# Two cross-attention layers on one core: eleven of layer 1's sixteen rotary chains are transposed by VectorE and on a way through DRAM

## The chip, the core and the metric

The kernel runs on one NeuronCore of a Trainium2 chip. A core has five engines that each work through a queue of their own in order: TensorE (PE, matrix products into PSUM), VectorE (DVE), ScalarE (ACT), GpSimd (POOL) and SyncE (SP), which here only issues DMA transfers. They wait for each other on semaphores. A DMA is waited for in the same way: whoever needs the data, or the buffer that a transfer reads, waits until it has landed. The metric is the device time of one execution in microseconds (us); a kernel is run several times and the median is taken.

## The reference

Four batches of 1024 rows pass through two cross-attention layers, everything in float32. Layer 0 normalises `x`, projects it to 16 heads of 64, attends to a context of 1024 rows and adds the projected result to `x`. Layer 1 does the same with 16 heads of 32, but its q and k are rotated and scaled to unit length before they meet:

```python
xn = x * rsqrt(mean(x * x) + EPS_RMS) * norm_w
q = (xn @ wq).reshape(B, T_dec, N_HEADS, HEAD_DIM)
k, v = split((encoder_out @ wkv).reshape(B, T_enc, 2, N_HEADS, HEAD_DIM))
q, k = rotate(q, cos, sin), rotate(k, cos, sin)
q, k = q / norm(q), k / norm(k)
attn = softmax(einsum("bqhd,bkhd->bhqk", q, k) * sqrt(HEAD_DIM))
out = residual + einsum("bhqk,bkhd->bqhd", attn, v).reshape(B, T_dec, D_Q) @ wout
```

## The kernel before, in words

The batches follow each other. In each, layer 0 works through eight pairs of heads (`Attention0`, L354), and then layer 1 through two halves of eight heads each (`Attention1`, L555). Everything that is not attention itself, such as projections, transposes and sums, is cut into units with an estimated PE cost in us. The `Units` object (L56) holds them in a list, and after each attention step `fill` (L70) issues as many as the step's share of cost allows, in the list's order. So the order of every engine's queue is settled when the program is built. A unit that costs 0.0 is issued as soon as it is reached while the step still owes time.

A half of layer 1 has 32 steps, counted here from 0 (steps of the second half go on from 32). A step (`att1.step`, L571) handles one block of 256 query columns, one group of four heads and two blocks of 128 keys: eight score matmuls (L581), two exps on ACT (L591) into one of two buffers, the eight products of the step before (L626), the units (`fill`, L595), and then two adds on VectorE that begin the softmax sums (L600), with a third (L602) in two of four steps. Each block of queries and group takes four steps; the second step of the next block holds the eight matmuls that end the sums (L645). A step's scores need the PSUM tiles of the step before, so its exps must be done. The query block changes every eight steps: steps 0, 8, 16 and 24 begin with columns 0, 256, 512 and 768 of q. PE writes two records for one such matmul, so that 16 records are eight matmuls.

Before they can meet in scores, q and k must lie with the head's dimension on partitions. `rotated_chains` (L452) makes them. A batch has sixteen chains: four each for k and q of the first half and of the second (`k`, `q` in the first, `k1`, `q1` in the second), each with 256 rows. A chain has three parts:

- `project` (L463): matmuls into one PSUM bank, rows on partitions; at the last, `rotate` (L475) is issued: a square on ACT (L478), five instructions on VectorE (L480 to L485), and on POOL the norm's inverse root (L487, L169) and the scaling (L491). The result is `t1`, 128 partitions x 512.
- nothing in the second place.
- `turn_over` (L494), cost 0.45: four PE transposes of 128x128 into a PSUM bank (L499) and one ACT copy into the q or k tile (L504).

`weave` (L96) puts a chain's turn two chains behind its projection. `t1` comes from `Scratch` (L525), which hands out four slots in turn, so a slot is written again four chains later. Marks (L859) make sure that the turns of q are issued before steps 8, 16 and 24 at the latest.

All DMA issues concerned here are on SP, in program order. During the first half of layer 1 SP has, before the change: the weights `wo1` for the second half (L863, `wo_load`, L653), then the next batch's weights `w` (L303) and context rows `c` (L176). The `wo1` weights are first used by the units `po1` in the fill of step 32, and the next batch's context rows in step 33 and after.

Of the kernel before, what the change touches and what calls it, by code (L numbers as in the profile page):

```python
# [29 lines left out]
F32 = mybir.dt.float32  # L33
AF = mybir.ActivationFunctionType
# [3 lines left out]
P = 128  # L38
S = 1024
NT = S // P  # L40
DQ = 512
NQ = DQ // P
DC = 384
NC_ = DC // P
# [4 lines left out]
HD1 = 32  # L49
# [60 lines left out]
def xattn_kernel(ctx: ExitStack, tc: tile.TileContext, a: dict, out: bass.AP):  # L110
    nc = tc.nc
    x, c = a["x"], a["ctx_768"]
# [3 lines left out]
    sb = ctx.enter_context(tc.tile_pool(name="sb", bufs=2))  # L116
    ps_s = ctx.enter_context(tc.tile_pool(name="ps_s", bufs=2, space=bass.MemoryType.PSUM))
    ps_f = ctx.enter_context(tc.tile_pool(name="ps_f", bufs=1, space=bass.MemoryType.PSUM))
    ctx.enter_context(tc.manual_schedule())

    def score(name, shape=(P, S)):
# [5 lines left out]
    def bank(name):  # L127

        while True:
            which["n"] = which["n"] + 1 if which["n"] < 3 else which["from"]  # L130
            if which["n"] != which["kept"]:
                break
            which["kept"] = None
        return ps_f.tile([P, 512], F32, tag=f"f{which['n']}", name=name)
# [25 lines left out]
    def matmul(o, lhsT, rhs, start, stop):  # L160

        w = P // which["cols"]
        for j in range(which["cols"]):
            rr = slice(j * w, (j + 1) * w)
            nc.tensor.matmul(o[rr], lhsT[:, rr], rhs, start=start, stop=stop)  # L165

    def rsqrt(o, v):

        nc.gpsimd.tensor_tensor(o, v, nhalf[:, : v.shape[1]], ALU.pow)  # L169
# [268 lines left out]
    TH = 2  # L438

    def half_kv_load(half, i):  # L440
        f0, f1 = half * FH, (half + 1) * FH
        w = sb.tile([P, NC_, FH], F32, tag=f"wkv{i}", bufs=1, name=f"wkv{i}_{half}")
        nc.sync.dma_start(w, a["wkv"][:, i * DQ + f0 : i * DQ + f1].rearrange("(n p) m -> p n m", p=P))
        return w

    def half_q_load(half):
        f0, f1 = half * FH, (half + 1) * FH
        wq = sb.tile([P, NQ, FH], F32, tag="wpair", bufs=2, name=f"wq1_{half}")
        nc.sync.dma_start(wq, a["wq"][:, f0:f1].rearrange("(n p) m -> p n m", p=P))
        return wq  # L450

    def rotated_chains(dst, src, nk, w, name, tmp):  # L452

        hd, nh = HD1 // 2, TH * FH // HD1
        tiles = {}

        def heads(ap):
            return ap.rearrange("p (t h d) -> p t h d", t=TH, d=HD1)

        def spread(ap):  # L460
            return ap.unsqueeze(2).to_broadcast([P, TH, FH // HD1, ap.shape[2]])

        def project(t0, i, k):  # L463
            if i == 0 and k == 0:
                tiles[t0] = [bank(f"{name}_p{t0}")]
                if which["from"] == 0:
                    which["kept"] = which["n"]
            pp = tiles[t0][0]
            t = t0 + i
            lhsT = src[t // 4][:, k, (t % 4) * P : (t % 4 + 1) * P]  # L470
            matmul(pp[:, i * FH : (i + 1) * FH], lhsT, w(k), k == 0, k == nk - 1)
            if i == TH - 1 and k == nk - 1:
                rotate(t0, pp)

        def rotate(t0, pp):  # L475

            t1, t2, sq = tmp.take()
            nc.scalar.activation(sq, pp, AF.Square)  # L478
            c_, s_ = cos[:, t0 : t0 + TH, :], sin[:, t0 : t0 + TH, :]
            nc.vector.tensor_mul(heads(t1), heads(pp), spread(c_))  # L480
            nc.vector.tensor_mul(heads(t2)[:, :, :, :hd], heads(pp)[:, :, :, hd:], spread(s_[:, :, :hd]))
            nc.vector.tensor_mul(heads(t2)[:, :, :, hd:], heads(pp)[:, :, :, :hd], spread(s_[:, :, hd:]))
            nc.vector.tensor_add(t1, t1, t2)
            ss = sb.tile([P, nh], F32, tag="ss", bufs=2, name=f"{name}_s{t0}")
            nc.vector.tensor_reduce(ss, sq.rearrange("p (h d) -> p h d", d=HD1), AX.X, ALU.add)  # L485
            sm = sb.tile([P, nh], F32, tag="sm", bufs=2, name=f"{name}_m{t0}")
            nc.gpsimd.tensor_scalar_max(sm, ss, EPS_L2 * EPS_L2)  # L487
            ri = sb.tile([P, nh], F32, tag="ri", bufs=2, name=f"{name}_r{t0}")
            rsqrt(ri, sm)
            t1h = t1.rearrange("p (h d) -> p h d", d=HD1)  # L490
            nc.gpsimd.tensor_mul(t1h, t1h, ri.unsqueeze(2).to_broadcast([P, nh, HD1]))  # L491
            tiles[t0] = t1

        def turn_over(t0):  # L494
            t1 = tiles.pop(t0)
            pt = bank(f"{name}_t{t0}")
            for g in range(2):
                for i in range(TH):
                    nc.tensor.transpose(  # L499
                        pt[:, (g * TH + i) * P : (g * TH + i + 1) * P],  # L500
                        t1[:, i * FH + g * P : i * FH + (g + 1) * P],
                        ident,
                    )
            nc.scalar.copy(dst()[:, :, t0 * P : (t0 + TH) * P], pt.rearrange("p (g t) -> p g t", g=2))  # L504

        return [
            (
                [(0.44, lambda t0=t0, i=i, k=k: project(t0, i, k)) for i in range(TH) for k in range(nk)],
                [],
                [(0.45, lambda t0=t0: turn_over(t0))],  # L510
            )
            for t0 in range(0, NT, TH)
        ]

    def qk_tile(name):
        return sb.tile([P, 2, S], F32, tag="qk", bufs=3, name=name)
# [196 lines left out]
    st, order = prepare_units(0)  # L713
# [14 lines left out]
    for b in range(B):  # L728
        ct, hT, pairs = st["ct"], st["hT"], st["pairs"]
# [6 lines left out]
        for p in range(NPAIR):  # L736
# [22 lines left out]
            if p == 6:  # L759
                kq = {}  # L760

                def begin(n, kq=kq, b=b):
                    kq[n] = qk_tile(f"{n}1_{b}_0")

                k = rotated_chains(lambda kq=kq: kq["k"], ct, NC_, lambda k, wk=wk: wk[:, k, :], f"k1_{b}_0", RowScratch())
                other = [(0.0, lambda: begin("k"))] + k[0][0] + flat(outs[:2]) + k[1][0] + k[0][2] + flat(outs[2:4])
            if p == NPAIR - 1:
# [4 lines left out]
                xnT = []  # L772
# [7 lines left out]
                wk1 = []  # L780
# [4 lines left out]
            n = 7 * (p == 0)  # L785
# [6 lines left out]
            if p == 5:  # L792
                wq = []
                work.add([(0.0, lambda wq=wq: wq.append(half_q_load(0)))])
            left = sum(c for c, _ in values) if p == NPAIR - 1 else 0.0
            for i in range(NT):
# [8 lines left out]
                n = NT * (NPAIR - p) - i  # L805
# [13 lines left out]
        tmp = Scratch(b)  # L819
        wv1, wq1 = half_kv_load(1, 1), half_q_load(1)  # L820
        begin("q")
        kT, qT = kq["k"], kq["q"]
        kT1, qT1 = qk_tile(f"k1_{b}_1"), sb.tile([P, 2, S], F32, tag="raw", bufs=1, name=f"q1_{b}_1")
        q = rotated_chains(lambda kq=kq: kq["q"], xnT, NQ, lambda k, wq=wq: wq[0][:, k, :], f"q1_{b}_0", tmp)
        k1 = rotated_chains(lambda kT1=kT1: kT1, ct, NC_, lambda k, wk1=wk1: wk1[0][:, k, :], f"k1_{b}_1", tmp)
        q1 = rotated_chains(lambda qT1=qT1: qT1, xnT, NQ, lambda k: wq1[:, k, :], f"q1_{b}_1", tmp)

        work.add(flat(outs[:4]) + norms[0]["stats"] + k1[0][0] + [(AV, att.product)] + norms[0]["apply"])
        work.add(norms[0]["turn"] + q[0][0] + k1[1][0] + k1[0][2] + [(AV, att.product)] + flat(outs[4:]) + q[0][2])
# [14 lines left out]
        for half in range(2):  # L844
            n = 0
# [14 lines left out]
            else:  # L860
# [4 lines left out]
                if b + 1 < B:  # L865
                    st, order = prepare_units(b + 1)
# [75 lines left out]
```

## Time and profile before

| | us |
|---|---|
| median of 3 runs | 2908.89 |
| lowest and highest run | 2907.53, 2913.90 |
| the profiled execution | 2903.31 |
| its span, first to last instruction | 2901.5 |
| PE busy in the span | 2849.7 |
| VectorE busy | 2189.1 |
| layer 1, first half, first batch | 497.65 to 624.34 |

The profile comes from one execution. It lists instructions by engine and line, with busy time and what ended the idle time ahead of them (`<-`). `PE q_t` and `PE k_t` are the transposes of `turn_over`, `q_p` and `k_p` the projections, `rot` is `t1` and its companions, `s` a score tile, `both` the softmax sums, `po` an output projection. A matmul's end is modelled, so start times of consecutive instructions tell more than durations. "SPq" rows are DMA issues. For a DMA the profile tells packets, bytes, and the time from issue to landing.

### The profile page before, as it was taken

The page shows a single profiled execution, that of the slowest core. Times are in us where ns is not written, and L with a number is a line of the kernel's source. Part 1 is how long each engine was busy: PE and PEld are TensorE (multiplying, and loading weights), DVE is VectorE, ACT ScalarE, POOL GpSimd, SP SyncE. Part 2 cuts the span into 40 slices and gives each one's busy share as a digit, 9 for nine tenths or more (in the row PEclk, how much of TensorE's full clock was granted, in tenths as well). Part 3 has the DMA queues.
Part 4 walks back from the last instruction along what each step waited for, and adds up shares of the span by engine and source line. Part 5 has one row for each costly group of instructions (what it writes and reads, how often), then busy time and mean ns, then how long its engine had stood idle before and what let it go on. Part 6 is the DMA issues. An engine that isn't in the chain of part 4 may idle for free.

```text
span 2901.5 us, 66687 instructions
## 1 busy us (share of the span) xinstructions
PE 2849.7 (98%) x27336; PEld 1425.7 (49%) x27336; DVE 2189.1 (75%) x2952; ACT 1439.5 (50%) x2329; POOL 938.9 (32%) x776
## 2 busy tenths in 40 slices
PE   8999999999999999999999999999999999999998
PEld 4444455555444444555544445455554444445544
DVE  5677785877777778587777777858877777786877
ACT  4444444666444444466644444446664444444665
POOL 2343353420134335432024433534102343353400
PEclk9999999999999999999999999999999999999999
DMA  5887775010398777401039887730104887773000
GB/s 144 189 187 181 167 171 133 22 37 25 75 210 192 183 170 175 113 22 36 26 92 211 192 184 166 178 93 22 36 26 112 207 197 183 165 171 81 2 2 30
DMA packets 177552, 348.87 MB, mean 120 GB/s; under 512 B 37600, under 2 KB 93152, under 8 KB 177248
## 3 DMA queue, kind: packets, MB, share of 16 engines
q1 hardware_dynamic: 175920, 343.96, 50.1%
q8 instruction: 216, 3.54, 0.5%
q14 instruction: 88, 0.72, 0.1%
q10 hardware_dynamic: 1328, 0.66, 0.1%
HBM read 67.64 MB, written 8.39 MB: 26 GB/s over the span
## 4 chain that ended last, share of the span: by engine, by line
PE 89%; DVE 4%; ACT 3%; issue 2%; SPq 1%; DMA 1%; POOL 1%; DVEq 0%; ACTq 0%
PE s L367 16%; PE av L428 15%; PE po L165 11%; PE s L581 9%; PE pv L165 8%; PE pqT L165 7%; PE av L626 7%; PE pkT L165 5%; PE q_p L165 4%; PE k_p L165 2%; PE av L645 2%; ACT e L591 1%; SPq L412 1%; PE pth L247 1%; DMA eT<-e 1%
## 5 line engine op out<-in xcount | busy, mean ns | idle before, releaser
L392 DVE TENSOR_REDUCE m<-s 128x1 f32<-128x1024 f32 x512 | 602.9, 1219 | 372.1 <-PE s L367 371.5
L591 ACT ACTIVATE e<-s 128x1024 f32<-128x1024 f32 x512 | 496.7, 1022 | 252.5 <-PE s L581 239.5
L398 POOL TENSOR_SCALAR raw<-raw,li 128x1024 f32<-128x1024 f32 x256 | 287.1, 1122 | 725.0 <-DVE li L397 717.0
L367 PE MATMUL s<-qk 64*128 64x512 f32 x2048 | 515.6, 615 | 2.9 <-ACT e L393 2.2
L393 ACT ACTIVATE e<-s,m 128x1024 f32<-128x1024 f32 x256 | 283.1, 1110 | 465.8 <-DVE m L392 224.2
L393 ACT ACTIVATE raw<-s,m 128x1024 f32<-128x1024 f32 x256 | 285.4, 1115 | 455.0 <-DVE m L392 455.0
L428 PE MATMUL av<-eT,v 128*64 128x256 f32 x4096 | 470.1, 382 | 4.8 <-DMA eT<-e 3.6
L398 POOL TENSOR_SCALAR e<-e,li 128x1024 f32<-128x1024 f32 x256 | 287.0, 1122 | 473.7 <-DVE li L397 244.2
L600 DVE TENSOR_TENSOR both<-e 128x512 f32<-128x512 f32 x512 | 340.5, 699 | 87.2 <-ACT e L591 84.3
L428 PEld LDWEIGHTS av<-eT,v 128*64 128x64 f32 x4096 | 284.7, 137 | 225.1 <-issue 84.8
L367 PEld LDWEIGHTS s<-qk 64*128 64x128 f32 x2048 | 183.7, 186 | 281.6 <-issue 165.9
L581 PE MATMUL s<-q,k 32*128 32x256 f32 x4096 | 306.0, 401 | 5.8 <-ACT q L504 2.7
L401 DVE STREAM_TRANSPOSE e<-e 128x1024 f32<-128x1024 f32 x256 | 310.0, 1229 | 0.3
L401 DVE STREAM_TRANSPOSE e<-raw 128x1024 f32<-128x1024 f32 x256 | 310.0, 1228 | 0.2 <-DMA eT<-e 0.2
L581 PEld LDWEIGHTS s<-q,k 32*128 32x128 f32 x4096 | 192.1, 184 | 141.0 <-ACT e L591 72.0
L165 PE MATMUL pqT<-hT,w 128*64 128x512 f32 (+1 forms) x1216 | 240.6, 595 | 2.5 <-ACT hT L249 2.5
L165 PE MATMUL po<-wo,vals 128*64 128x512 f32 x1024 | 234.6, 596 | 0.0
L295 DVE TENSOR_TENSOR x<-x,po 128x512 f32<-128x512 f32 x200 | 131.7, 678 | 86.2 <-PE po L165 85.2
L165 PEld LDWEIGHTS pv<-w,cT 128*64 128x64 f32 (+1 forms) x3360 | 170.3, 132 | 41.6 <-issue 34.8
L165 PE MATMUL pv<-w,cT 128*64 128x128 f32 (+1 forms) x3360 | 184.3, 274 | 0.7 <-ACT hT L249 0.7
L165 PE MATMUL pkT<-cT,w 128*64 128x512 f32 (+1 forms) x912 | 182.4, 598 | 0.0
L602 DVE TENSOR_TENSOR both<-both 128x1024 f32<-128x1024 f32 x128 | 159.7, 1248 | 4.4
(82 smaller groups left out, 2776.1 us busy)
## 6 DMA issues: line engine op xcount, KB each, us to landing
eT<-e SPq DMA_DIRECT2D x2048, 128.0 KB, 2.4
xr<-in_x_dram SPq DMA_DIRECT2D x32, 256.0 KB, 4.0
wo<-in_Wo_dram SPq DMA_DIRECT2D x16, 512.0 KB, 4.5
x<-in_x_dram SPq DMA_DIRECT2D x32, 256.0 KB, 4.0
out_dram<-x SPq DMA_DIRECT2D x32, 256.0 KB, 2.6
w<-in_Wq_dram SPq DMA_DIRECT2D x31, 256.0 KB, 3.2
c<-in_ctx_dram SPq DMA_DIRECT2D x32, 192.0 KB, 4.2
wkv<-in_wkv_dram SPq DMA_DIRECT2D x16, 384.0 KB, 3.5
```

Source lines behind the costliest of these rows:

```text
L165: nc.tensor.matmul(o[rr], lhsT[:, rr], rhs, start=start, stop=stop)
L367: nc.tensor.matmul(sc[j][:, kb * 512 : (kb + 1) * 512], pr["qT"][r[j], i * P : (i + 1) * P], pr["kT"][r[j], kb * 512 : (kb + 1) * 512], st ...
L392: nc.vector.tensor_reduce(m[:, j : j + 1], sc[j], AX.X, ALU.max, negate=True)
L393: nc.scalar.activation(e[j], sc[j].rearrange("p (g s) -> p g s", g=4), AF.Exp, bias=m[:, j : j + 1], accum_out=l[:, j : j + 1])
L398: nc.gpsimd.tensor_scalar(e[j], e[j], li[:, j : j + 1], HD0**-0.5, ALU.mult, ALU.mult)
L401: self.turn = [lambda j=j: nc.vector.transpose(self.e[:, :, i % BQ * 2 + j, :], e[j]) for j in range(2)]
L428: nc.tensor.matmul(av[r[j], :W].rearrange("p (t a i) -> p t a i", t=BQ, a=4), pr["v"][:, k, r[j]], eT[:, j, :, :, k * 32 : (k + 1) * 32], ...
L581: nc.tensor.matmul(sc[j // 2][:, j % 2, c, :], kT[rr, g, k * P : (k + 1) * P], qT[rr, g, qb * WQ : (qb + 1) * WQ], start=True, stop=True,)
L591: nc.scalar.activation(e, sc[u], AF.Exp, scale=float(np.sqrt(np.float32(HD1))))
L600: nc.vector.tensor_add(into[:, 2 * u : 2 * u + 2, :], es[u][:, :, 0, :], es[u][:, :, 1, :])
L602: nc.vector.tensor_add(acc, acc, into)
L626: nc.tensor.matmul(self.av[rr, 0, :], v[g][:, 2 * kk + c, rr], es[j // 2][:, j % 2, c, :], start=first and c == 0, stop=end and c == 1,)
```

## The change

`rotated_chains` takes a new argument, `blocks_from`. Chains whose first row block is at or behind it have a new turn. All four `k1`, all four `q1` and the last three `q` chains of a batch have it: eleven of sixteen, 44 in all. The five others (the four of `k` and the first of `q`) keep `turn_over`.

For the eleven, `rotate` writes its result with heads ahead of row blocks, which changes access patterns only. The turn has two units of cost 0.0. `turn_blocks` transposes `t1` in place in 32x32 blocks on VectorE, and writes it to a DRAM tile in four transfers, one for each group of 32 partitions, in pieces of 32 elements. `put_blocks` reads it back into the q or k tile in four transfers, one for each head of the four, in pieces of 256 elements. All eight are issued by SP. There are four DRAM tiles in turn. PE and ACT have no part in it.

```diff
+    dram = ctx.enter_context(tc.tile_pool(name="dram", bufs=4, space=bass.MemoryType.DRAM))
...
-    def rotated_chains(dst, src, nk, w, name, tmp):
+    def rotated_chains(dst, src, nk, w, name, tmp, blocks_from=NT):
...
-        def heads(ap):
-            return ap.rearrange("p (t h d) -> p t h d", t=TH, d=HD1)
+        def heads(ap, t0=-1):
+
+            order = "p (h t d) -> p t h d" if t0 >= blocks_from else "p (t h d) -> p t h d"
+            return ap.rearrange(order, t=TH, d=HD1)
...
-            nc.scalar.activation(sq, pp, AF.Square)
+            nc.scalar.activation(heads(sq, t0), heads(pp), AF.Square)
...
-            nc.vector.tensor_mul(heads(t1), heads(pp), spread(c_))
-            nc.vector.tensor_mul(heads(t2)[:, :, :, :hd], heads(pp)[:, :, :, hd:], spread(s_[:, :, :hd]))
-            nc.vector.tensor_mul(heads(t2)[:, :, :, hd:], heads(pp)[:, :, :, :hd], spread(s_[:, :, hd:]))
+            h1, h2 = heads(t1, t0), heads(t2, t0)
+            nc.vector.tensor_mul(h1, heads(pp), spread(c_))
+            nc.vector.tensor_mul(h2[:, :, :, :hd], heads(pp)[:, :, :, hd:], spread(s_[:, :, :hd]))
+            nc.vector.tensor_mul(h2[:, :, :, hd:], heads(pp)[:, :, :, :hd], spread(s_[:, :, hd:]))
...
+        def turn_blocks(t0):
+            t1 = tiles.pop(t0)
+            nc.vector.transpose(t1, t1)
+            way = dram.tile([HD1, 2, 4, TH, P], F32, tag="way", name=f"{name}_w{t0}")
+            for a in range(4):
+                to = way.rearrange("d g h t (a x) -> a d (g h t) x", a=4)[a]
+                nc.sync.dma_start(to, t1[32 * a : 32 * (a + 1)].rearrange("d (n x) -> d n x", x=32))
+            tiles[t0] = way
+
+        def put_blocks(t0):
+            way = tiles.pop(t0)
+            for h in range(4):
+                to = dst()[32 * h : 32 * (h + 1), :, t0 * P : (t0 + TH) * P]
+                nc.sync.dma_start(to, way[:, :, h].rearrange("d g t x -> d g (t x)"))
+
...
-                [(0.45, lambda t0=t0: turn_over(t0))],
+                [(0.0, lambda t0=t0: turn_blocks(t0)), (0.0, lambda t0=t0: put_blocks(t0))]
+                if t0 >= blocks_from
+                else [(0.45, lambda t0=t0: turn_over(t0))],
...
-        q = rotated_chains(lambda kq=kq: kq["q"], xnT, NQ, lambda k, wq=wq: wq[0][:, k, :], f"q1_{b}_0", tmp)
-        k1 = rotated_chains(lambda kT1=kT1: kT1, ct, NC_, lambda k, wk1=wk1: wk1[0][:, k, :], f"k1_{b}_1", tmp)
-        q1 = rotated_chains(lambda qT1=qT1: qT1, xnT, NQ, lambda k: wq1[:, k, :], f"q1_{b}_1", tmp)
+        q = rotated_chains(lambda kq=kq: kq["q"], xnT, NQ, lambda k, wq=wq: wq[0][:, k, :], f"q1_{b}_0", tmp, TH)
+        k1 = rotated_chains(lambda kT1=kT1: kT1, ct, NC_, lambda k, wk1=wk1: wk1[0][:, k, :], f"k1_{b}_1", tmp, 0)
+        q1 = rotated_chains(lambda qT1=qT1: qT1, xnT, NQ, lambda k: wq1[:, k, :], f"q1_{b}_1", tmp, 0)
```

## The prediction, made before the changed kernel had run

> **What bounds the kernel now.** I read the busy table first, then the chain of waits, then the timeline of layer 1's first half in the first batch.
>
> ```profile
> PE 2849.7 (98%) x27336; PEld 1425.7 (49%) x27336; DVE 2189.1 (75%) x2952; ACT 1439.5 (50%) x2329; POOL 938.9 (32%) x776
> ...
> PE 89%; DVE 4%; ACT 3%; issue 2%; SPq 1%; DMA 1%; POOL 1%; DVEq 0%; ACTq 0%
> ```
>
> PE sets the end. In layer 1 it is no different: from 564 to 626 us PE is busy 61.96 of 62 us, DVE 53.32, and the DMA engines 2%. So a PE instruction taken out is time gained, and a microsecond in which PE waits is time lost.
>
> ```profile
> 555.47 1.15 PE L581 MATMUL s<-q,k 32*128 32x256 f32 x16
> ...
> 558.41 0.66 PE L499 MATMUL q_t<-ident,rot 128*128 128x128 f32 x4
> 558.54 0.60 ACT L478 ACTIVATE rot<-q_p 128x512 f32<-128x512 f32 x1
> ...
> 558.99 1.15 PE L581 MATMUL s<-q,k 32*128 32x256 f32 x16
> ...
> 559.17 0.69 DVE L480 TENSOR_TENSOR rot<-q_p,cos 128x512 f32<-128x512 f32 x1 [1.46 <-ACT rot L478]
> ...
> 560.17 1.94 ACT L591 ACTIVATE e<-s 128x1024 f32<-128x1024 f32 x2 [0.49 <-PE s L581]
> ...
> 561.17 0.68 DVE L485 TENSOR_REDUCE q_s<-rot 128x16 f32<-128x512 f32 x1
> ...
> 562.36 1.15 PE L581 MATMUL s<-q,k 32*128 32x256 f32 x16
> ```
>
> These are steps 14, 15 and 16 (scores at 555.47, 558.99, 562.36). The transposes at 558.41 make the q columns that step 16 reads; they delay the next score by 0.58 us and are ready 3 us early. SP's queue:
>
> ```profile
> 477.84 18.96 SPq L655 DMA_DIRECT2D wo<-in_wout_dram  x2
> ...
> 558.54 0.37 SPq L307 DMA_DIRECT2D w<-in_Wk_dram  x1
> ...
> 560.10 3.52 SPq L182 DMA_DIRECT2D c<-in_ctx_dram  x4
> ```
>
> The weights `wo1` of the second half, first used at 626 us, are issued by 497: SP has nothing else in between, so it runs 130 us ahead.
>
> **What the change removes.** 44 chains (11 in each of 4 batches) lose four PE transposes and an ACT copy. PE: 44 x 0.59 us (540.78 to 541.37 for one set) = 26.0 us. One set had waited 1.43 us for POOL (at 515.67, and the same at 1232.71); VectorE now waits in its place: 4 x 1.43 = 5.7. **Gain 31.7 us.** The copies (44 x 0.59) lie on ACT at 50% and count nothing.
>
> **What it adds on VectorE.** 44 transposes of 128x512; L401 takes 1229 ns for 128x1024, so 0.61 us each, 27 us in all. They lie beside PE while VectorE is about 85% busy; by themselves 0, at worst the same 27. The rotary writes in another order keep their sizes; rows of two operands and 128x512 take 678 to 699 ns in every layout here (L295, L480, L600), so I take 0 (44 x 0.02 either way is 1 us).
>
> **What one way through DRAM takes.** All eight transfers are issued by SP, in order. An issue costs about 0.5 us (0.37 to 0.59). Four writes carry 512 pieces of 128 B each, 2048 in all. The trace has no such transfer. Nearest are the weight loads, with nothing beside them:
>
> ```profile
> DMA packets 1329, 0.67 MB, mean 96 GB/s; under 512 B 48, under 2 KB 1328, under 8 KB 1328
> ...
> q1 hardware_dynamic: 1328, 0.66, 33.1%
> ...
> w<-in_Wq_dram SPq DMA_DIRECT2D x1, 256.0 KB, 4.1
> ...
> w<-in_Wv_dram SPq DMA_DIRECT2D x1, 192.0 KB, 4.0
> ```
>
> That is 720 to 727 us: 33.1% of 16 engines over 7 us for 1328 packets, 28 ns a packet, and 5.0 us from the first issue (720.64) to the last landing (721.61 + 4.0), of which 1328/16 x 28 ns = 2.3 is packets and 2.7 the rest. For 2048 packets: 2.7 + 3.6 = 6.3 if a packet costs the same whatever its size, 2.7 + 0.9 = 3.6 if it goes by bytes, and 1.5 + 7.5 = 9.0 by the longest landing of an `eT` block. I take **W = 6.0**, near the first. Reads (1 KB pieces, 256 packets): the last issue 1.5 after the first, landing like `eT` in 2.4: **R = 3.9** (3.5 to 4.6). A read waits for all four writes, so SP is held W + 4 x 0.5 = **8.0 us** a chain (5.3 to 11), and data are there 9.9 us after the transpose.
>
> The Trainium skill, "DMA: Bandwidth & Descriptors", Specifications, says that transfers below 512 B are read-modify-writes. No row here has one; if that doubled the 28 ns, W would be 9.9, beyond my upper end, and it speaks against this change.
>
> **Where PE waits for it.** I set the order of the two built programs side by side; it is the same in all four batches. A step is 1.08 (scores) + 1.00 (products) + 1.29 (12 filler matmuls) = 3.37 us, and 0.86 more for the sums of every fourth. Exps end 3.12 after the scores begin (558.99 to 562.11). A rotation is 0.63 for the square until VectorE starts, and 2.68 there (559.17 to 561.85). s15 is the start of step 15.
>
> - *Step 16*, reading q columns 512 to 767. The turn has cost 0 now, the fill rates sink, and this turn moves from step 14 to the end of step 15, behind the rotation of the next q chain on VectorE. Its transpose ends at s15 + 3.12 + 0.63 + 2.68 + 0.61 = 7.04, data land at 16.9; PE is ready at 1.08 + 1.00 + 12 matmuls = 3.37. **13.6 us**, and everything on PE is behind it. Ends: 7.04 + 7.1 - 3.37 = 10.8 and 7.04 + 13.6 - 3.37 = 17.3.
> - *Step 24*. The chain before it on SP (k1, turned in step 18 after a rotation and the sums' adds) is ready at s18 + 6.45 and holds SP to 14.45; q lands at 24.35, s24 is at 6 x 3.37 + 0.86 = 21.1. **3.3 us** (0 to 10).
> - *Step 32*. SP reaches `wo1` only behind the last three q1 chains, turned in steps 28, 30 and after 31. They are closer than 8.0 us, so they queue: the first is ready at s28 + 5.2, the third done at 5.2 + 24 = 29.2, and `wo1` lands 4.2 later (row of the issues) at 33.4. PE wants it at 4 x 3.37 + 0.86 + 2.08 = 16.4. **17.0 us** (5.2 + 15.9 + 4.0 - 16.4 = 8.7 to 26). The next batch's weights and context rows stand behind `wo1` in SP; they land some 5 us after it, about when PE, itself late, asks for them: 0.
> - *VectorE in step 12*: the k1 rotation takes the scratch slot whose writes began at s10 + 7.04 and land at 13.0; it could start at 10.5. VectorE holds the adds behind it, ACT's exp waits for the adds, PE for the exp: **2 us** (0 to 5).
> - *Step 8*: ready at s4 + 4.27 (POOL) + 0.61 + 9.9 = 14.8, needed at 15.0: **0** (to 3.5).
>
> Sum 35.9 a batch, 144 us.
>
> **A cold PE.** In the first microseconds, after 3.75 us without work, 12 records of `pkT` took 4.12 us; the next 12 took 2.80, both at a granted clock of 1.00. I charge each of the eight long waits this 1.3: 10 us (0 to 20).
>
> The Trainium skill, "TensorE: Matmul & The Clock Gate", Part 1, gives half rate after an idle window of about 3.4 us until as long a busy one. An estimate by it is 1.7 us lost each time, 14 in place of 10.
>
> **The sum.** +144 + 10 - 31.7 = +122 us on the profiled execution's 2903.3 (span 2901.5): 3026. That execution lies 5.6 under the median of 2908.89 and 4.2 under the lowest run shown, so the changed kernel's median may lie as much above 3026; the range has room for it. Low ends: 4 x (10.8 + 0 + 8.7 + 0 + 0) = 78 - 32 = +46: 2950. High ends: 4 x (17.3 + 10 + 26 + 5 + 3.5) = 247 + 10 - 26 = +231: 3135.
>
> **The rivals.**
> - *The waits are hidden and PE's gain stays: faster.* 2903.3 - 31.7 = 2872. It needs step 16's data by s15 + 3.4, and `wo1` before step 32. For it: PE is at 98% and the DMA engines at 2% here. Against it: the rotation ahead of the transpose alone ends at 6.4. It decides only if VectorE could transpose before that rotation, which the order denies. 5%.
> - *Only step 16 waits*: SP drains its chains in under 4 us each, so that `wo1` is in time: 4 x 13.6 + 5 - 32 = +27: 2930. For it: an `eT` transfer lands in 2.4. Against it: eight issues alone take 4 us. 8%.
> - *VectorE becomes the bound of the first half*, its 27 us all on the path, beside the waits: 3053. It is within my range; 15%.
> - *Small pieces cost far more* than the longest landing: over 3135, 5%.
>
> **How the numbers follow.** Forecast 65%, time 3026. The range reaches from just above rival two to the high end, 2945 to 3130, holding 8 in 10. A measurement can tell about 0.2% (6 us) from no change. Faster is rival one, 5%; a time between it and rival two, within 0.2%, has 2%; slower is the forecast and the other three, 65 + 8 + 15 + 5 = 93%.
>
> **What would show it.** Right: PE idle before the scores released by a DMA, four times about 14 us, and before `po` released by a DMA of `wo`, four times about 17; SP's `wo1` issue at the end of the first half instead of before it; writes landing 4 to 6 us after their first issue; PE transposes `q_t` and `k_t` down from 256 to 80. Wrong: a `wo1` that lands before step 32 takes away 68 us; W of 4 instead of 6 takes away some 53 (2 + 3.3 + 6 + 2 a batch); a VectorE that never idles in the first half shows rival three.

## The result and the profile after

| | before | after |
|---|---|---|
| median of 4 runs, us | 2910.77 | 3017.89 |
| lowest and highest run | 2907.53, 2913.90 | 3010.69, 3021.02 |
| the profiled execution, and its span | 2903.31, 2901.5 | 3010.69, 3008.9 |

The ratio is 1.0365, with a 95% interval from 1.0348 to 1.0383: the change costs 3.7%. The forecast was 3026 us. Between the profiled executions the difference is 107.4 us; 122 had been forecast. The busy row and the chain of waits of the changed kernel:

```profile
PE 2855.5 (95%) x27160; PEld 1427.9 (47%) x27160; DVE 2214.5 (74%) x2996; ACT 1419.4 (47%) x2285; POOL 924.6 (31%) x776
...
PE 77%; DVE 8%; DMA 6%; SPq 4%; ACT 3%; issue 2%; POOL 0%; ACTq 0%; DVEq 0%
```

PE falls from 98% to 95% of a longer span, and DMA and SP's queue, 1% each before, now carry 10% of the chain that ended last. The waits of PE tell who stands there (us in total, times, longest):

```profile
PE po L167 <- DMA wo<-in_wout_dram: 57.8, 4, 15.3
PE s L605 <- DMA q<-q_w: 49.0, 8, 11.7
```

Neither row was there before. They are the two waits that the prediction named, once a batch each: 15.3 us for `wo1` (17.0 forecast), and 11.7 for the turn at step 16 (13.6 forecast), with under 1 us at step 24 in the same row. PE's timeline of the first batch, steps 16 and 32 (start, us, ..., idle time before and its releaser):

```profile
568.20 3.75 PE L605 MATMUL s<-q,k 32*128 32x256 f32 x16 [11.73 <-DMA q<-q_w]
571.88 1.94 PE L650 MATMUL av<-e,v 128*32 128x256 f32 x16
573.59 1.86 PE L167 MATMUL q_p<-wq,hT 128*32 128x256 f32 x24
...
650.61 3.64 PE L167 MATMUL po<-wo,o 128*32 128x512 f32 x16 [15.34 <-DMA wo<-in_wout_dram]
```

The three rows after the first wait take 3.75, 1.94 and 1.86 us, where undisturbed they take 1.15, 1.07 and 1.48. Two things are in that. The windows of the same stretch show the clock (the first number after the engines' busy times):

```profile
560.00:562.00 2.00, 0.00 (x0) 0.00 (x0) 2.00 (x5) 0.00 (x0) 1.11 (x2) 0.68 0.00 0
562.00:574.00 12.00, 5.80 (x36) 3.72 (x40) 1.90 (x3) 2.06 (x3) 3.13 (x2) 0.50 0.22 44
574.00:576.00 2.00, 2.00 (x40) 1.04 (x32) 0.00 (x0) 0.25 (x1) 0.00 (x0) 0.91 0.00 0
```

If the clock is either 1 or the 0.50 of the second row, a mean of 0.68 over 2 us is 0.72 us at 1 and 1.28 at half: it went to half at 560.7, 4.3 us after PE had run out of work (556.5). In the same way 0.91 is 0.36 us at half and puts its return at 574.4, 6.2 us after PE had begun again. The other thing is that the four read transfers land some 0.6 us apart, head by head (568.06, 568.61, 569.24, 569.84), and each group of scores waits for its own. VectorE and SP's queue show where the wait came from:

```profile
560.64 0.70 DVE L515 STREAM_TRANSPOSE rot<-rot 128x512 f32<-128x512 f32 x1
```

```profile
561.37 2.59 SPq L519 DMA_DIRECT2D q_w<-rot  x4
565.66 2.48 SPq L526 DMA_DIRECT2D q<-q_w  x4
...
623.05 2.60 SPq L519 DMA_DIRECT2D q_w<-rot  x4
628.74 2.48 SPq L526 DMA_DIRECT2D q<-q_w  x4
631.26 2.60 SPq L519 DMA_DIRECT2D q_w<-rot  x4
637.02 2.48 SPq L526 DMA_DIRECT2D q<-q_w  x4
639.55 2.60 SPq L519 DMA_DIRECT2D q_w<-rot  x4
643.91 2.48 SPq L526 DMA_DIRECT2D q<-q_w  x4
646.43 1.10 SPq L679 DMA_DIRECT2D wo<-in_wout_dram  x2
```

From the first write's issue to the first read's is W = 4.3 us, and the reads take 2.5 more: SP is held 6.8 us by this chain. For the last q1 chains W is 5.7, 5.8 and 4.4. These three follow each other without a gap from 623 to 646, 7.8 us each, and `wo1`, issued by 497 before the change, stands behind them.

For the rest of this document I cut layer 1 at the starts of scores, and sum the four batches of the profiled execution (us; "rest" is layer 0 and the ends):

| steps | 0-16 | 16-17 | 17-24 | 24-26 | 26-32 | 32-40 | 40-63 | rest |
|---|---|---|---|---|---|---|---|---|
| before | 258.9 | 18.7 | 104.3 | 31.4 | 93.5 | 122.2 | 355.1 | 1917.4 |
| after | 282.3 | 32.9 | 100.0 | 39.6 | 90.3 | 188.6 | 355.1 | 1920.1 |

### The profile page after: what moved, and what is told of

It reads as the page before. It is cut to its first block, busy times and chain, and to the rows that moved or that the text cites. A ratio compares the mean times of both kernels' runs of the same rounds, so it can differ in the third digit from the quotient of the medians.

```text
span 3008.9 us, 66884 instructions
## 1 busy us (share of the span) xinstructions
PE 2855.5 (95%) x27160; PEld 1427.9 (47%) x27160; DVE 2214.5 (74%) x2996; ACT 1419.4 (47%) x2285; POOL 924.6 (31%) x776
## 4 chain that ended last, share of the span: by engine, by line
PE 77%; DVE 8%; DMA 6%; SPq 4%; ACT 3%; issue 2%; POOL 0%; ACTq 0%; DVEq 0%
PE s L369 15%; PE av L430 14%; PE po L167 10%; PE pqT L167 7%; PE s L605 7%; PE pv L167 7%; PE pkT L167 5%; PE av L650 5%; PE k_p L167 2%; DVE both L624 2%; SPq L414 2%; PE q_p L167 2%; PE av L669 2%; DMA q_w<-rot 2%; ACT e L615 2%
## 5 line engine op out<-in xcount | busy, mean ns | idle before, releaser
L605 PE MATMUL s<-q,k 32*128 32x256 f32 x4096 | 322.6, 407 | 56.6 <-DMA q<-q_w 49.0
L605 PEld LDWEIGHTS s<-q,k 32*128 32x128 f32 x4096 | 203.3, 186 | 199.9 <-ACT e L615 91.8
L167 PE MATMUL po<-wo,o 128*32 128x512 f32 (+1 forms) x824 | 130.8, 628 | 60.8 <-DMA wo<-in_wout_dram 57.8
```

The costliest lines, as they stand in the source:

```text
L605: nc.tensor.matmul(sc[j // 2][:, j % 2, c, :], kT[rr, g, k * P : (k + 1) * P], qT[rr, g, qb * WQ : (qb + 1) * WQ], start=True, stop=True,)
```

## The experiments

All ratios are against the kernel before, run on the same chip. **My theory**: two waits a batch, one for the turn behind a rotation, one for loads behind SP's chains, and a half clock after each. **Rivals**: VectorE bounds the first half; the way through DRAM is too slow wherever it is put; the clock plays no part.

**The output weights alone.** The load of `wo1` is moved from the start of the second half to that of the first:

```diff
+        wo1 = [wo_load(a["wout"], i, f"wo1_{b}_{i}") for i in range(2)]
         for half in range(2):
...
-                wo1 = [wo_load(a["wout"], i, f"wo1_{b}_{i}") for i in range(2)]
```

> Against the changed kernel's 3017.9 us. It issues the second half's output weights (wo1) before the first half, ahead of all chains in SP's queue; everything else stays. My theory (two waits a batch, at step 16 for the turn behind a rotation and at step 32 for loads that stand behind SP's chains, and some 3.5 us at half clock after each): the wait of po at step 32 goes (4 x 15.3), but the next batch's weights and context rows still stand behind the same chains, so PE waits for them in step 33 instead, in three of four batches, about 13 to 14 us each: a gain of 15.3 + 3.5 in the last batch and 1 to 3 in the others, 20 to 30 us, 2988 to 2998, with waits of PE for a DMA of c or w in the place of those for wo. Rival (only wo1 is late, the other loads land in time as my prediction's 0 for them says): 4 x 18.8 = 75 us, 2943. Rival (VectorE or the DMA way itself bounds the first half): no gain, 3018.

2999.8 us, 1.0302 (1.0284 to 1.0319). Waits of PE in that kernel:

```profile
PE s L605 <- DMA q<-q_w: 49.6, 9, 11.9
PE ptc L193 <- DMA c<-in_ctx_dram: 44.1, 7, 13.2
```

The row for `wo` is gone, and the next batch's context rows wait in its place, 13.2 us, as the theory says: they stood behind the same chains and had been covered by PE's own wait. Steps 32 to 40 fall from 188.6 to 167.1, 14.8 of the 21.5 us in the last batch, which has no next one.

**The other loads too.** The next batch's key weights and first four context loads are issued ahead of the last q1 chains as well, behind the second value chain:

```diff
+                i = rest.index(vs[1])
+                rest[i] = (vs[1][0] + ahead_st["early"], [], [])
```

> As the run before it, and the next batch's key weights and first four context loads are issued early too, about step 19, ahead of the last q1 chains in SP's queue. My theory: all of the wait at step 32 goes and nothing takes its place: 4 x (15.3 + 3.5) = 75 us, about 2943, with only the four waits of the scores at step 16 left (11.7 each). Rival (VectorE bounds the first half, or the chains of q1 themselves land late): the wait of PE comes back in step 32 as one for the q or k tile or for VectorE, 2990 or more.

2988.8 us, 1.0254 (1.0227 to 1.0281): a miss by 46 us. Steps 32 to 40 fall to 137.1, so the theory of that wait holds, but steps 17 to 26 rise from 139.6 to 160.8. The timeline of PE has a new wait at step 24:

```profile
609.93 3.88 PE L605 MATMUL s<-q,k 32*128 32x256 f32 x16 [5.27 <-DMA q<-q_w]
```

In my edit the loads came before the last q chain's turn in SP's queue. Its writes were issued at 601.16, its reads at 607.49: W was 6.3 behind 1.4 MB of loads in the same queue.

**The order alone.** The third and fourth q chains go ahead of two k1 chains, and the third is turned one chain after its projection:

```diff
-                first = [..., (norms[1]["apply"], [], k1[1][2]), k1[2]]
-                rest = [(norms[1]["turn"] + q[2][0], [], q[2][2]), k1[3], q[3], q1[0], ...]
+                first = [..., (norms[1]["apply"], [], k1[1][2])]
+                rest = [(norms[1]["turn"] + q[2][0], q[2][2], []), q[3], k1[2], k1[3], q1[0], ...]
```

> The loads stay as in the changed kernel. The projections of the third and fourth q chain come ahead of the last two k1 chains, and the third q chain's turn follows its own rotation at once, so that its data are asked for several steps before step 16. My theory: the wait at step 16 goes, 4 x (11.7 + 0.6 + 3.5) = 63 us, about 2955, and the wait for wo at step 32 stays at about 15. Rival (the way through DRAM is simply too slow or VectorE too busy, wherever the turn is put): the wait moves to step 16 or 24 in another size, 3000 to 3018.

3011.3 us, 1.0338 (1.0323 to 1.0354): a miss by 56, and the rival's number. The wait for `q_w` is gone, but steps 0 to 16 take the same 282.3. VectorE was not too busy there; it stood still. Its timeline, and PE's after it:

```profile
552.98 1.29 DVE L515 STREAM_TRANSPOSE rot<-rot 128x512 f32<-128x512 f32 x2
...
566.76 0.69 DVE L487 TENSOR_TENSOR rot<-k_p,cos 128x512 f32<-128x512 f32 x1 [7.96 <-DMA k_w<-rot]
```

```profile
571.22 2.99 PE L605 MATMUL s<-q,k 32*128 32x256 f32 x16 [4.98 <-ACT e L615]
```

Two chains were transposed together and went through SP one behind the other; the slot of the second came free only when its writes had landed, and the next rotation needed that slot. VectorE stood 7.96 us, behind it the adds, behind them the exp, behind it PE. It is the prediction's chain for step 12, in another step and four times the size.

**The clock.** Unused matmuls fill the time in which PE waits (24 ahead of step 16, 32 ahead of the units of step 32):

```diff
+                nc.tensor.matmul(pp[:, :256], ident, cos.rearrange("p t d -> p (t d)"), start=True, stop=True)
```

> The changed kernel with extra work: 24 unused matmuls of 128x256 (0.43 us each at full clock, some 10 us) ahead of step 16's scores and 32 (some 14 us) ahead of the units of step 32, in each batch, which only fill the time in which PE waits anyway; the output does not depend on them. My theory: the waits end when they ended before, but PE comes out of them at full clock, so 8 times 3.4 = 27 us are gained, about 2991, and the granted clock in the profile stays near 1.0 over the waits. Rival (the clock records do not show in the time, or the cause of the lost time after the waits is another): 3018 or more; by the 1.3 us of my prediction it would be 10 us, 3008.

3010.9 us, 1.0335 (1.0320 to 1.0351); 7 us gained of the 27 expected. In the first batch the clock stayed at 1.00 over step 16, and steps 16 to 17 took 6.14 us instead of 8.04: 1.9 us is what the clock costs there. In the other three it fell nevertheless, and the same steps took 7.64, 7.77 and 9.20 us instead of 7.90, 8.11 and 8.84. The scores of step 16 in the first and the last batch, and the clock in the last (0.97, then 0.50):

```profile
571.19 3.05 PE L605 MATMUL s<-q,k 32*128 32x256 f32 x16 [1.08 <-DMA q<-q_w]
```

```profile
2802.45 4.01 PE L605 MATMUL s<-q,k 32*128 32x256 f32 x16 [0.94 <-DMA q<-q_w]
```

```profile
2802.00:2804.00 2.00, 1.44 (x5) 0.86 (x6) 0.00 (x0) 0.00 (x0) 0.00 (x0) 0.97 0.32 98
2804.00:2806.00 2.00, 2.00 (x12) 1.36 (x11) 0.00 (x0) 0.32 (x1) 0.00 (x0) 0.50 0.00 0
```

At full clock the sixteen records still take 3.05 us instead of 1.15: 1.9 us are the four heads that land in turn, about 0.6 us apart. So of the 3.5 us that I had charged to the clock after a wait, about half is the wait itself, going on; and PE that works in pieces while the heads come in loses its clock without any long pause. In the first batch more than that gain went back by step 24, whose data land at a time that SP sets: PE waited there 1.30 us instead of 0.95 and now lost its clock (0.50 from 606 to 608), and steps 17 to 26 took 37.3 us instead of 34.3. After the waits of step 32 the clock stayed at 1.00 in all four batches, and the first 16 records of `po` took 1.92 us instead of 3.64 in the first; yet steps 32 to 40 fell by only 3.8 us in all, to 184.8.

**Early chains and more slots.** Value chains, which have no rotation, go between the q chains, the k1 chains come later, and the scratch has six slots for `t1`:

```diff
-            return self.t[:, self.n % 4], self.t[:, 4 + self.n % 2], self.t[:, 6 + self.n % 2]
+            return self.t[:, self.n % 6], self.t[:, 6], self.t[:, 7]
...
+                first = [q[1], (norms[1]["stats"], [], []), vs[0], (norms[1]["apply"], [], k1[1][2]), vs[1]]
+                rest = [(norms[1]["turn"] + q[2][0], [], q[2][2]), vs[2], q[3], k1[2], k1[3], q1[0], q1[1], q1[2]]
+                rest += [q1[3], vs[3]]
```

> The loads stay as in the changed kernel (3017.9 us). The third and fourth q chain come early, with value chains (which have no rotation) between them and the k1 chains behind them, and six scratch slots for the turned tile are made out of the eight rows that are there (one each is left for the two other intermediates). The run with only the order changed had shown that the wait for the way at step 16 went and that one for a scratch slot came in its place, 7.96 us of VectorE for the writes of a k1 chain. My theory now (SP's serial way holds the slot until its writes land; with more slots and earlier chains nothing is late in step 16 or 24): steps 0 to 16 go from 70.6 to about 60 us, steps 16 to 26 lose another 5, some 4 x 15 = 60 us, 2958; the wait of step 32 stays or grows, since six k1 and q1 chains now run one behind the other on SP, 2955 to 2985. Rival (VectorE is the bound of the first half): steps 0 to 16 stay near 70, 3010 or more.

3052.7 us, 1.0483 (1.0468 to 1.0499): slower than the change itself. Steps 0 to 16 stay at 69.1 us a batch, as the rival has it, but the trace names another reason: the wait for a slot is gone, and the third q chain, whose turn I had left two chains behind its projection, is again behind the fourth's rotation (PE waits up to 10.5 us for it at step 16). The k1 and q1 chains, moved back, end later, and PE waits 23.2 us for `wo1` instead of 15.3.

**The same with early loads**, this time behind the last q chain's turn:

```diff
+                rest[rest.index(q1[0])] = (ahead_st["early"] + q1[0][0], [], q1[0][2])
```

> As the run before it, with the second half's output weights issued ahead of the first half and the next batch's key weights and first context loads right behind the turn of the last q chain, ahead of all q1 chains in SP's queue (in the earlier try they stood ahead of that turn, and step 24 waited 5.27 us for it). My theory: no long wait is left, PE keeps its clock, and the gain of the transposes shows: 2911 - 31.7 = 2879, up to 2900 if the loads still cost the 2.6 us at the start of each half that both earlier runs with them showed. Rival (VectorE bounds the first half, its 31 us of transposes on the path): 2911 or more. Rival (the q1 chains, now last, are late themselves): a wait of the scores in step 32 for a q or k tile, 2911 to 2950.

2991.8 us, 1.0275 (1.0260 to 1.0290). My 2879 to 2900 is missed by far; it lies in the first rival's "2911 or more", but the two long waits that are left in PE's timeline are for DMAs, not for VectorE:

```profile
568.48 3.95 PE L605 MATMUL s<-q,k 32*128 32x256 f32 x16 [10.28 <-DMA q<-q_w]
...
660.11 0.97 PE L193 MATMUL ptc<-ident,c 128*128 128x128 f32 x2 [10.52 <-DMA c<-in_ctx_dram]
```

The first is the third q chain. The second is the next batch's *second* four context loads: their slots come free only in step 33, and they stood behind the last q1 chain in SP (issued at 657.37).

**VectorE's price.** Each transpose is done three times:

```diff
+            for _ in range(3):
+                nc.vector.transpose(t1, t1)
```

> The changed kernel with each VectorE transpose done three times in place (which leaves the same data as once): 88 more instructions of 0.70 us, 62 us of VectorE. My theory (VectorE is not the bound, but its transposes stand in the chain that ends in the wait of step 16): 2 x 0.70 more in each of the four waits of step 16 and as much at most at step 24 and 32, 6 to 17 us more than the changed kernel, 3024 to 3035. Rival (VectorE bounds the first half): the whole 62, 3080. Rival (only SP's queue and the transfers count): 3018.

3054.5 us, 1.0490 (1.0473 to 1.0508): 36.6 us more than the change, between my 6 to 17 and the rival's 62. The wait of step 16 grew by 2.1 to 13.8 us, that for `wo` by 1.4, but steps 0 to 16, with the first of these in them, by 4.3: VectorE has less room than its 74% says, and 0.59 of each microsecond added to it comes through.

**Only k1 and q1 through DRAM**, with the early loads; the q chains are turned by PE:

```diff
-        q = rotated_chains(..., f"q1_{b}_0", tmp, TH)
+        q = rotated_chains(..., f"q1_{b}_0", tmp)
```

> As the second run of this call, but the three q chains are turned by PE again, so that eight chains a batch go through DRAM (k1 and q1, which have until step 32): 12 sets of PE transposes of 0.59 come back, 7 us. My theory: 7 us slower than that run if it has no wait left, so about 2886; faster than it where that run still waits in step 16 or 24.

2947.2 us, 1.0123 (1.0108 to 1.0138): not the 2886 without a wait, but faster than the run before, which still waited at step 16. Steps 0 to 16 take 245.0, 13.9 less than before the change; what is left is the wait for the second context loads, up to 10.0 us in three batches.

**Those loads on ScalarE's queue**, with eight chains and with all eleven, the third q chain now turned one chain after its projection:

```diff
-                nc.sync.dma_start(raws[t], ...)
+                (nc.scalar if b and h else nc.sync).dma_start(raws[t], ...)
```

> The kernel in which k1 and q1 alone (eight chains a batch) go through DRAM, output weights and first loads early, with one more edit: the next batch's second four context loads, which need slots that come free only in step 33, are issued by ScalarE instead of standing behind the q1 chains in SP's queue. In that kernel PE still waited 10.0 us for them in step 33 to 34 (three batches), and steps 34 to 40 took 37 us instead of 22.7; all other stages were within 3 us of the kernel before. My theory (SP's order is the last thing that is late): that wait goes, 3 x 13 = 39 us off 2947, about 2908, within 0.3% of the kernel before or up to 0.5% faster (8 chains x 4 x 0.59 = 19 us of PE gained, some of it given back as short waits for VectorE). Rival (another resource, such as the q1 tiles, is late at the same place): 2935 or more.

> All eleven chains through DRAM, as in the run with early chains and early loads, with the same edit for the second context loads, and with the third q chain turned one chain after its projection instead of two (there it was projected by step 10, but turned only behind the fourth one's rotation at 561 us, and step 16 waited 10.3 us). My theory: both waits go, 3 x 13 + 4 x 13 = 91 off 2992, about 2901 to 2910; steps 0 to 16 take 59 to 62 us. Rival (the way is too slow for q in any place, or VectorE bounds): steps 0 to 16 stay near 69, 2945 or more.

Eight chains: 2916.5 us, 1.0009 (0.9997 to 1.0020). Eleven: 2910.1 us, 0.9998 (0.9987 to 1.0009). The whole 3.7% is gone in both, with the way through DRAM kept. Steps 0 to 16 take 235.4 with eleven chains, 23.5 less than before the change, but steps 32 to 40 still 133.6. ScalarE there, its four issues taken by themselves (ns: shortest, median, longest), and PE:

```profile
628.56 4.36 ACTq L184 DMA_DIRECT2D c<-in_ctx_dram  x3
633.02 1.94 ACT L615 ACTIVATE e<-s 128x1024 f32<-128x1024 f32 x2 [3.98 <-DVE x L297]
```

```profile
L184 ACTq DMA_DIRECT2D c<-in_ctx_dram x4: 334/388/501, 628.2 to 632.6; - x4
```

```profile
634.10 0.70 PE L605 MATMUL s<-q,k 32*128 32x256 f32 x4 [1.98 <-ACT e L615]
```

No issue takes more than 0.50 us; the 4.36 us of the last three are mostly the time between them. The trace's semaphore records show what ScalarE stood for: the third and the fourth issue wait for semaphores that two writes of a q1 chain set, and begin within 0.1 us of the landing of these writes, at 629.28 and 632.51 (at 635.54 and 639.38 in the run with eight chains). So the way through DRAM held ScalarE's queue too. The exp stands behind the fourth issue, begins after 3.98 us of idle time, and PE waits 1.98 us for it. (The releaser named is VectorE's last instruction before it. But in the run with eleven chains and these loads on SP, where VectorE does the same at this place, the longest wait of the scores for an exp is 0.3 us, so I take it to be ScalarE's own queue.)

**Late turns, and a control.** The context loads are on SP again, and the turns of the last two q1 chains, not read before steps 48 and 56, go behind them into the second half. The control has all these edits, but turns all sixteen chains by PE:

```diff
+                late = q1[2][2] + q1[3][2]
+                rest = rest[:-1] + [(q1[2][0], [], []), (q1[3][0], [], []), vs[3]]
...
+                    cts[1]["load"] + late + some(1) + cts[1]["turn"],
```

> All eleven chains through DRAM, as in the last run but for two edits: the second four context loads are on SP again (on ScalarE their issue held the exp behind them 4 us, and PE waited 2 us and lost its clock), and the turns of the last two q1 chains, whose columns are read only from steps 48 and 56 on, are issued in the second half behind those loads. My theory (the way through DRAM costs nothing once no load and no step stands behind it): the 4.4 us that steps 34 to 40 still lost in three batches go, 3 x 4.4 = 13 off about 2910, 2897 or 0.5% under the kernel before; steps 0 to 32 stay at 122.7 against 126.7. Rival (VectorE, which was busy without a break at the end of the first half, holds the exps there whatever the loads do): 2908 or more, no gain.

> A control: every edit of the run beside it (early chains, six scratch slots, early loads, late turns), but all sixteen chains turned by PE and copied by ScalarE as in the kernel before. My theory: what the way through DRAM itself brings is the difference of the two, at most 44 x 0.59 = 26 us; if the other edits are worth nothing by themselves, this run stands at the kernel before, 2908 to 2916, and the run beside it 10 to 26 under it. Rival (the gain of the run beside it, if it has one, comes from order and early loads): this run is as fast as it or faster.

Eleven chains through DRAM: 2899.9 us, 0.9962 (0.9948 to 0.9977). The control: 2896.9 us, 0.9943 (0.9931 to 0.9956). Both beat the kernel before, and they can't be told from each other. Steps 32 to 40 take 123.0, so the wait for the exp is gone with the loads back on SP (but also with two transposes of VectorE moved away; the run does not part the two). By stage:

| steps | 0-16 | 16-17 | 17-24 | 24-26 | 26-32 | 32-40 | 40-63 | rest |
|---|---|---|---|---|---|---|---|---|
| eleven, late turns | 235.4 | 22.2 | 106.3 | 32.7 | 94.3 | 123.0 | 357.0 | 1918.6 |
| control | 244.8 | 18.0 | 106.6 | 33.3 | 89.3 | 124.3 | 353.3 | 1921.7 |

PE's waits of the first half, first batch, in the one with DRAM, in the control, and in the kernel before:

```profile
PE av L669 <- DVE both L624: 2.9, 3, 1.5
```

```profile
PE q_t L506 <- POOL rot L498: 1.0, 1, 1.0
```

```profile
PE pth L247 <- DVE rot L482: 1.5, 1, 1.5
PE q_t L499 <- POOL rot L491: 1.4, 1, 1.4
```

So the rival holds: the gain comes from order and early loads, not from the way through DRAM. Without a long wait left, DRAM saves 9.4 us in steps 0 to 16 against the control. It loses 4.2 at step 16, 5.0 in steps 26 to 32 and 3.7 in steps 40 to 63. Of waits, the sums' matmuls stand for VectorE's adds 2.9 us a batch, 11.6 in all, most of it in steps 17 to 32. By the busy rows of PE the transposes take 28.6 us less than in the control (13.1 for 41.7), but scores and sums 18.5 more (391.2 for 372.7). Why these do can't be read off, since the filler between steps is shared out differently in the two and a matmul's end is modelled; how PE's 26 us went stays open. So does which of its edits brings the control's 14 us in steps 0 to 16; 1.9 us a batch are the two waits of the kernel before that shrank to one.

## Why the prediction was right, and where it was off

- *Direction and mechanism*: right. Both big waits stand where the order had put them, released by the DMAs named, and the runs with loads and chains moved took them away and brought them back. PE transposes are 80, VectorE idles in each long wait.
- *Step 16*, 13.6 forecast: 11.73 to the first head and 1.9 more to the last, 13.6. That the sum is right is luck, since its terms cancel: the transpose ends 8.3 us after step 15's start instead of 7.04 (VectorE takes the adds first, and 0.70 instead of 0.61), W is 4.3 instead of 6.0, and the reads end some 4.2 after their first issue.
- *W = 6.0*: the term that was mis-sized. It was 4.2 to 4.6 us in 34 of the 44 chains; in the other ten it was 4.9 to 5.9, six of them in the last q1 chains (one write of the chain at 623 us took 3.9 us to land). Why they did stays open. I took the time of a packet from weight loads, 28 ns. The stretch from 561 to 566 us of the changed kernel, with nothing beside the writes and the first read, says:

```profile
DMA packets 2112, 0.26 MB, mean 52 GB/s; under 512 B 2112, under 2 KB 2112, under 8 KB 2112
...
q1 hardware_dynamic: 2112, 0.26, 32.9%
```

  32.9% of 16 engines over 5 us for 2112 packets is 12.5 ns each, between the 28 ns of an equal time for each packet and the 7 ns of an equal time for each byte. For most chains the low end of 3.6 was the better neighbour. The Trainium skill, "DMA: Bandwidth & Descriptors", Specifications, has transfers below 512 B as read-modify-writes; the doubling of the 28 ns that I had put beside it does not show here, at 128 B, and whether such a write is in the 12.5 ns no run tells.
- *Step 32*, 17.0: at most 15.3 and 14.5 in the mean (57.8 / 4). In the first batch SP was as slow as forecast: three chains in 23.4 us (24 forecast), and `po` starts with its weights 33.3 us after step 28 (33.4 forecast). PE was late itself, at 18.0 instead of 16.4, since step 28 with its sums took 5.7 us instead of 4.2. In the last batch the three chains took 20.9 us, and the wait was 12.6. *Step 24*, 3.3: the stage from 24 to 26 grew by 8.2 / 4 = 2.1. *The slot at step 12*, 2: nothing on PE. The rotation did begin only when the last write had landed (545.60 after 545.37), but with the short W that was less than 1 us late; the order experiment found this wait at 7.96. These three more than make up the 15 us by which the forecast was high: steps 32 to 40 grew by 66.4 instead of 4 x (17.0 + 1.3) = 73.2, steps 24 to 26 by 8.2 instead of 13.2, and the slot's 8 are absent on PE, 19.8 in all; step 16 (60.8 with its clock instead of 59.6), the gain (30.7 instead of 31.7) and the rest (2.7 instead of 0) were 4.9 low.
- *Cold PE*, 1.3 a wait: 1.9 in the one batch where it could be taken out, and 32.9 - 18.7 = 14.2 us in the four step 16s together with the heads' landing. The rows that gave 1.3 had a granted clock of 1.00, so they measured something else. "TensorE: Matmul & The Clock Gate", Part 1, of the Trainium skill led to 1.7, nearer. Its windows of some 3.4 us run freely, by the same part, so a fall 4.3 us after PE stopped and a return 6.2 us after it began again, in pieces at first, do not contradict them; but I had not expected the fall in the filled run, with no pause over 1 us in sight.
- *The next batch's loads at 0*: right as put, since PE was late itself; 13.2 us as soon as it wasn't.
- *PE's gain of 31.7*: the stages without a long wait shrank by 23.2 (steps 0 to 16, less the 46.6 by which the four step 15s were over 3.37) + 4.3 + 3.2 = 30.7. Right in this kernel, as a remainder; but the control shows that it is not a gain that better order would have kept.
- *VectorE's 27 us at 0*: too low as a price, not decisive for this result. It was a rival at 15%; 0.59 us came through for each one added, where I had looked only at its busy share.

## What to carry to other kernels

A queue that waits for its own transfers is a resource with a hold time: list all that stands behind it, loads for much later included, and move those first. Taking away the last late thing shows the next one (`wo1`, then the first context rows, then the second four, then the exp behind a DMA issue that waited for a chain's write), so cost a cure by the next in line, not by the wait that it removes. And run the cure without the change as a control: here order and early loads alone gave all of the gain.

## What the runs showed of the chip that I had not expected

- Four writes of 512 pieces of 128 B, 64 KB each, landed 2.2 us after their issue in the median and 4.0 at most; 12.5 ns a packet where nothing ran beside them.
- The granted clock went to 0.50 some 2.4 us after dense work had ended (last batch of the filled run), where PE paused 0.94 us and then worked in pieces, as the heads landed, and stayed there 6.8 us.
- Four DMA issues of context rows held ScalarE's queue from 628.2 to 632.9 us, though each took 0.33 to 0.50: two of them waited for another queue's transfers to land.
- A VectorE transpose of 128x512 took 0.70 us in place, more than half of the 1.23 for 128x1024.
